# Two groups of four routed choices by 26 block products, in place of four pairs

## The chip, the cores and the metric

One core of a Trainium2 chip runs the kernel. Time is the device time of one execution in microseconds (us). The engines are named as in the profile: PE (TensorE, matmuls), PEld (its weight loads), DVE (VectorE), ACT (ScalarE), POOL (GpSimd) and SP (the queue that issues most DMAs). L738 means line 738 of the kernel before.

## The reference: what is computed

Sixteen batches of 256 rows and 256 columns pass two layers, each added to its input, all in float32.

- Layer 0: each batch takes the one expert of eight with the largest entry of `cond_8`: `silu(x Wu + bu) * (x Wg + bg)`, 512 wide, then back to 256 columns.
- Layer 1: each batch takes its two best experts of eight, weighted, and a shared one: `gelu(x Wg) * (x Wu)`, 1024 wide, then back to 256 columns.

```python
w, sel = jax.lax.top_k(softmax(router_logits), 2)
w = w / w.sum(axis=-1, keepdims=True)
...
out = sum over experts of we[:, None, None] * _gemma_mlp(x, g, u, d)
out = out + _gemma_mlp(x, shared_gate, shared_up, shared_down)
```

So layer 1 has 32 routed choices (16 batches, two each) and 16 batches for the shared expert.

## The kernel before

**Units.** The choices are sorted by expert on the chip, so that two neighbours of one expert form a *pair*. A `Pair` multiplies the expert's weights, cut in 2 x 2 blocks, with the two batches by seven block products in place of eight (`STEPS`, numbered 0 to 6). Its up part has four *quarters* (j = 0 to 3) in layer 1, each with seven products of two matmuls (gate and up, m = 0 and 1): 14 matmuls, at L753. Its down part has seven steps of four matmuls (L839), which are spread over the quarters of the next unit. A `Single` handles one choice without any scheme. A `Quad` handles four batches of one expert: its up part is two times 26 block products (`BLOCK`) of two matmuls, at L1126, and its down part is that of two pairs (its `halves`). Before the change only the shared expert's last twelve batches are done by quads, three of them; the other four shared batches are two pairs.

**Order in layer 1.** Two shared pairs, then the routed pairs (twelve that are always there, and up to four further ones, as many as the routing gives, chosen in a switch with one arm for each number), a single, the three quads, and the last single.

**A quarter of a pair.** Products 0, 2 and 4 sum in one PSUM bank, X. After each, ACT copies the bank to SBUF (u1, u2, u3; `copy`, L730), and PE may not add the next of them before the copy has read the bank. DVE combines such copies with the other banks into four blocks, C11 after product 1, C22 after 4, C21 after 5, and C12 after product 6, which is recorded in the next quarter (`combine`, L738). Then come GELU on ACT (L795), the product on DVE (L801), and three sums of the result on DVE (`sums_b`, L681 to L683). POOL makes four sums of each quarter's weights (`sums_a`, L688 to L691) three quarters ahead into `s` buffers, and once in a pair four sums of the down weights. POOL also issues the DMAs that add results to `out` (L650). SP loads weights (`q`) five quarters ahead.

**The written order.** All instructions are recorded in an order fixed by hand: a clock advances two units for each of the first six products of a quarter (`line.main`), so twelve units make a quarter, and `line.later(n, f)` records `f` when the clock has gone n units on. What falls due between two products is recorded between them, on whatever engines it uses. Each engine runs its own instructions in that order and waits by semaphores for others.

**Preparation.** A quad needs 26 factors for each half of the weights: P0 to P3 (blocks), Q0 to Q3 (blocks plus multiples of them, `RATIOS` = -1, 0, 1, 2), and for each two i < j a W (difference of two Q over the difference of their ratios) and two N (a block less W). `prepare()` makes them once, for the shared expert, among the routed pairs, and writes them to DRAM (`factors`), from where the quads load them. Its pieces are recorded 5 clock units into quarters j = 0 and 1 of the pairs after the first: `load` brings 1 MB of weights into the tile `spare` (L1326), `sums_w` makes Q (POOL, L1336), `pair` makes W and two N (POOL at L1346, L1350 and L1351, 256 elements wide; ACT scales W at L1349 where the ratios differ by more than one), `store` writes 128 KB at a time (L1321). The results pass through a ring of eight 256-wide pieces of the tiles `z`, `xs0` and `xs1`.

**Down weights of the quads.** All three quads use one expert's down weights `d` and their sums `ds` (L839 reads both), loaded once for the first of them.

**Sorting.** `order_by_expert` gives every choice a key, its expert times 32 plus its index; choices that are left over from pairs get 4096 more, and so come last.

Of the kernel before, what the change touches and what calls it, by code (L numbers as in the profile page):

```python
# [17 lines left out]
P = 128  # L18
# [6 lines left out]
NP2 = (NA - E) // 2  # L25
NS1, NS2 = B - 1 - 2 * NP1, NA - 2 * NP2
# [42 lines left out]
QUADS = (B - 2 * NF) // 4  # L69
# [5 lines left out]
def kernel(  # L75
# [22 lines left out]
    factors = [dram.tile([P, QW], F32, name=f"factors{j}") for j in range(CHUNKS)]  # L98

    qsums = [dram.tile([P, QW], F32, name=f"qsums{j}") for j in range(KPS[1])]  # L100
    dsums = dram.tile([P, 4 * KPS[1] * P], F32, name="dsums")
# [299 lines left out]
    def order_by_expert(v, g):  # L401
# [11 lines left out]
        odd, key, batch = map(small, ("odd", "key", "batch"))  # L413
        ri = small("ri", dt=I32)
# [31 lines left out]
        v.tensor_copy(ri, rank)  # L446
        v.tensor_single_scalar(ri, ri, 1, ALU.bitwise_and)
        v.tensor_copy(odd, ri)
        step(v)
        v.tensor_tensor(count, count, odd, ALU.add)  # L450
# [212 lines left out]
    class Pair(Unit):  # L663
# [41 lines left out]
        def sums_d(self):  # L705
            s = take("ds", 4, KPS[1], P, of=self)
            self.ds = s[:, :, : self.kp]
            flat = s.rearrange("p k j h -> p (k j h)")
            if self.at is None and self is not shared[0]:
                nc.sync.dma_start(flat, dsums)  # L710
                return
            d, s = self.d, self.ds
            self.sums_a(lambda n: d[:, A_AT[n]], lambda n: s[:, S_AT[n]])
            if self is shared[0]:
                nc.gpsimd.dma_start(dsums, flat)
# [236 lines left out]
    class Quad(Unit):  # L952
# [6 lines left out]
        def __init__(self, n, at, batches_at):  # L959
            super().__init__(n, 1, at, batches_at)  # L960
            self.kp = CHUNKS
            self.halves = [Pair(next(names), 1, at, batches_at[i : i + 2]) for i in (0, 2)]
# [3 lines left out]
        def load_q(self, j, behind=False):  # L966
            t = take("q", QB)[:, :QW]
            nc.sync.dma_start(t, factors[j])
# [58 lines left out]
        def load_d(self):  # L1027
            self.d = take("d", DW, of="quads")[:, : 4 * self.kd * P]
            src = wd1[bass.ds(self.expert(), 1)].rearrange("e p f -> (e p) f")
# [5 lines left out]
        def sums_d(self):  # L1035
            self.ds = take("ds", 4, self.kd, P, of="quads")
            nc.sync.dma_start(self.ds.rearrange("p k j h -> p (k j h)"), dsums)
# [55 lines left out]
        def down_over(self, h):  # L1093
# [3 lines left out]
            if h is self.halves[0]:  # L1097
                for sums in self.second:
                    sums()
            if not h.last:  # L1100
# [85 lines left out]
        def down(self, h, k):  # L1186
            h.d, h.ds = first_quad.d, first_quad.ds
            h.down(k)

    class Single(Unit):  # L1190
        width = 1

        def up(self, j):
# [31 lines left out]
            self.acts.append(act)  # L1225

        def down(self, j):
# [16 lines left out]
            if self.layer:  # L1244
# [7 lines left out]
                if self.x_from:  # L1252
# [13 lines left out]
        def piece(self, line, j, among=False):  # L1266
# [5 lines left out]
            if self.layer:  # L1272
                line.later(SINGLE_UP + 4 * bool(self.x_from), lambda: self.down(j))
# [34 lines left out]
    def prepare():  # L1308
# [3 lines left out]
        p = []  # L1312
        raw = {}
        ring = [areas["z"][:, i * S : (i + 1) * S] for i in range(4)]
        ring += [areas[f"xs{i}"][:, k * S : (k + 1) * S] for i in range(2) for k in range(2)]
        at = iter(range(1000))

        def store(g, name, src):
            n = g * len(BLOCK) + BLOCK.index(name)
            dst = factors[n // FACTORS][:, n % FACTORS * S : (n % FACTORS + 1) * S]  # L1320
            nc.sync.dma_start(dst.rearrange("p (m h) -> p m h", m=2), src)  # L1321

        def load(g):
            t = areas["spare"].rearrange("p (j m k h) -> p j m k h", j=2, m=2, k=4)
            for j in range(2):
                nc.sync.dma_start(areas["spare"][:, bass.ts(j, QW)], wq1[E, 2 * g + j])  # L1326
            for i in range(4):
                j, half = divmod(i, 2)
                raw["u", i], raw["w", i] = (t[:, j, :, 2 * half + c, :] for c in range(2))

        def sums_w(g):
            tt = nc.gpsimd.tensor_tensor
            for i, k in enumerate(RATIOS):
                w, u = raw["w", i], raw["u", i]
                for _ in range(abs(k)):
                    tt(w, w, u, ALU.add if k > 0 else ALU.subtract)  # L1336

        def store_w(g):
            for i in range(4):
                store(g, f"P{i}", raw["u", i])  # L1340
                store(g, f"Q{i}", raw["w", i])

        def pair(g, i, j):
            tt = nc.gpsimd.tensor_tensor
            t = [ring[next(at) % 8].rearrange("p (m h) -> p m h", m=2) for _ in range(3)]
            tt(t[0], raw["w", j], raw["w", i], ALU.subtract)  # L1346
            d = RATIOS[j] - RATIOS[i]
            if d != 1:
                nc.scalar.activation(t[0], t[0], AF.Copy, scale=1.0 / d)  # L1349
            tt(t[1], raw["u", i], t[0], ALU.subtract)  # L1350
            tt(t[2], raw["u", j], t[0], ALU.subtract)  # L1351
            raw[i, j] = t

        def store_pair(g, i, j):
            for name, t in zip((f"W{i}{j}", f"N{i}{j}", f"N{j}{i}"), raw[i, j]):
                store(g, name, t)

        for g in range(2):
            p += [[partial(load, g)], [partial(sums_w, g)]]
            ij = [(i, j) for i in range(4) for j in range(i + 1, 4)]  # L1360
            after = [partial(store_w, g)]
            for i, j in ij:
                p.append([*after, partial(pair, g, i, j)])
                after = [partial(store_pair, g, i, j)]
            p.append(after)
# [7 lines left out]
    quads = [Quad(next(names), None, range(i, i + 4)) for i in range(2 * NF, B, 4)]  # L1373
    first_quad = quads[0]
    first_quad.x_at = None
    pairs = [Pair(next(names), 1, 2 * i) for i in range(NP2)]
# [362 lines left out]
```

## Time and profile before

| | us |
|---|---|
| median of three runs | 1032.93 (1032.56 to 1033.51) |
| the profiled execution, whole | 1031.96 |
| its span in the trace | 1030.4 |
| PE busy in the span | 1022.7 (4714 matmul instructions) |
| DVE, POOL and ACT busy | 779.7, 499.3 and 384.5 |
| moved by DMA | 151.16 MB, 147 GB/s on average |

A row of a group reads: line, engine, operation, tile written <- tiles read, shapes (partitions x elements), count; then busy time, mean ns of one, and the engine's idle time just before with what ended it. A row of a timeline reads: start, length, engine, line, operation, tiles, count, and in brackets the idle time before it with what ended it. The granted clock of TensorE was full in every stage of this run.

### The profile page before, as it was taken

How to read it: one execution, taken by the hardware profiler on the slowest of the kernel's cores; microseconds unless marked ns; L12 is line 12 of the kernel's file. 1: busy time of each engine (PE TensorE's matmuls, PEld its weight loads, DVE VectorE, ACT ScalarE, POOL GpSimd, SP SyncE). 2: the span in 40 equal slices, each digit the busy share in tenths (PEclk: the TensorE clock that was granted, in tenths of full speed). 3: DMA queues.
4: the chain of work that ended last, by engine and by line, in shares of the span. 5: the costliest groups of instructions: out<-in, count | busy, mean ns of one | idle time of the engine just before them, and what ended most of it. 6: DMA issues, size and time to landing. Idle time of an engine off the chain costs nothing.

```text
span 1030.4 us, 14361 instructions
## 1 busy us (share of the span) xinstructions
PE 1022.7 (99%) x4714; PEld 894.1 (87%) x4714; DVE 779.7 (76%) x1265; ACT 384.5 (37%) x626; POOL 499.3 (48%) x558
## 2 busy tenths in 40 slices
PE   9999999999999999999999999999999999999998
PEld 7888888888888888888888888888888888888887
DVE  7888998777778778777887777777752897787661
ACT  2444443333333333333333333333331563543310
POOL 3929842455866977785887557647300000000001
PEclk9999999999999999999999999999999999999999
DMA  7635657552572464365346415423445653643324
GB/s 238 236 106 188 232 194 272 218 138 98 154 199 98 118 174 140 130 176 164 107 118 174 106 60 175 132 102 103 132 139 139 203 184 102 164 123 96 114 47 76
DMA packets 70027, 151.16 MB, mean 147 GB/s; under 512 B 8114, under 2 KB 39730, under 8 KB 66994
## 3 DMA queue, kind: packets, MB, share of 16 engines
q1 hardware_dynamic: 56674, 134.61, 38.6%
q0 software_dynamic: 12976, 15.21, 10.0%
q8 instruction: 42, 0.69, 0.3%
q14 instruction: 47, 0.39, 0.1%
q10 hardware_dynamic: 288, 0.26, 0.1%
HBM read 119.13 MB, written 30.93 MB: 146 GB/s over the span
## 4 chain that ended last, share of the span: by engine, by line
PE 96%; DVE 2%; DMA 1%; ACT 0%; issue 0%; SPq 0%; DVEq 0%
PE bank L753 46%; PE bank L839 31%; PE bank L1126 13%; PE bank L1199 4%; PE bank L1232 2%; DMA bt<-x_dram 1%; DVE c L738 1%; PE bank L231 1%; DVE bt L801 0%; DVE bt L681 0%; ACT c L789 0%; DVE bt L682 0%; PE bank L424 0%; ACT cp L730 0%; ACT c L795 0%
## 5 line engine op out<-in xcount | busy, mean ns | idle before, releaser
L730 ACT ACTIVATE cp<-bank 128x512 f32<-128x512 f32 x246 | 146.6, 596 | 382.7 <-PE bank L753 382.7
L753 PE MATMUL bank<-xt,s 128*128 128x256 f32 x1088 | 257.6, 380 | 0.4 <-DVE c L738 0.4
L738 DVE TENSOR_TENSOR c<-cp,bank 128x512 f32<-128x512 f32 x328 | 212.2, 679 | 26.2 <-ACT cp L730 16.2
L753 PEld LDWEIGHTS bank<-xt,s 128*128 128x128 f32 x1088 | 206.7, 190 | 29.2 <-DVE c L738 1.1
L753 PE MATMUL bank<-xt,q 128*128 128x256 f32 x816 | 195.8, 379 | 0.0
L650 POOL DMA_DIRECT2D out_dram<-ys x46 | 49.7, 1172 | 301.1 <-DVE ys L875 183.3
L839 PE MATMUL bank<-bt,ds 128*128 128x256 f32 x800 | 192.6, 380 | 0.0
L753 PEld LDWEIGHTS bank<-xt,q 128*128 128x128 f32 x816 | 155.3, 190 | 20.8
L801 DVE TENSOR_TENSOR bt<-c 128x1024 f32<-128x1024 f32 x82 | 115.4, 1407 | 76.5 <-ACT c L795 76.0
L839 PEld LDWEIGHTS bank<-bt,ds 128*128 128x128 f32 x800 | 152.0, 190 | 21.1 <-issue 0.7
L839 PE MATMUL bank<-bt,d 128*128 128x256 f32 x564 | 135.1, 379 | 0.0
L839 PEld LDWEIGHTS bank<-bt,d 128*128 128x128 f32 x564 | 107.3, 190 | 14.4
L688 POOL TENSOR_TENSOR s<-q 128x256 f32<-128x256 f32 x78 | 78.6, 1008 | 74.3 <-PE bank L753 45.2
L691 POOL TENSOR_TENSOR s<-s,q 128x256 f32<-128x256 f32 x78 | 66.8, 857 | 66.7 <-PE bank L753 64.0
L681 DVE TENSOR_TENSOR bt<-bt 128x512 f32<-128x512 f32 x101 | 81.3, 805 | 2.5 <-DMA bt<-x_dram 2.4
L689 POOL TENSOR_TENSOR s<-s,q 128x256 f32<-128x256 f32 x78 | 76.3, 978 | 6.1
L1126 PE MATMUL bank<-xt,q 128*128 128x256 f32 x336 | 77.0, 380 | 0.2 <-DVE ds L1151 0.2
L690 POOL TENSOR_TENSOR s<-q 128x256 f32<-128x256 f32 x78 | 74.0, 949 | 0.2 <-PE bank L753 0.2
L795 ACT ACTIVATE c<-c 128x1024 f32<-128x1024 f32 x68 | 71.5, 1051 | 6.8 <-DVE c L738 6.8
L1126 PEld LDWEIGHTS bank<-xt,q 128*128 128x128 f32 x336 | 63.8, 190 | 9.3 <-DVE ds L1151 0.6
L1126 PE MATMUL bank<-s,q 128*128 128x256 f32 x288 | 66.4, 379 | 0.0
L683 DVE TENSOR_TENSOR bt<-bt 128x256 f32<-128x256 f32 x94 | 61.4, 653 | 3.2
(225 smaller groups left out, 1121.2 us busy)
## 6 DMA issues: line engine op xcount, KB each, us to landing
q<-wq_dram SPq DMA_DIRECT2D x90, 512.0 KB, 3.7
q<-factors SPq DMA_DIRECT2D x39, 512.0 KB, 3.4
d<-wd_dram SPq DMA_DIRECT2D x17, 1024.0 KB, 5.8
xt<-x1d SPq DMA_DIRECT2D x46, 256.0 KB, 5.0
out_dram<-ys POOLq DMA_DIRECT2D x46, 256.0 KB, 5.8
d<-wd_dram SPq DMA_DIRECT2D x7, 513.0 KB, 3.8
bt<-x_dram SPq DMA_DIRECT2D x14, 256.0 KB, 5.1
x1d<-ys SPq DMA_DIRECT2D x14, 256.0 KB, 4.0
```

What stands on the lines that cost most here:

```text
L681: tt(more[:, 0:2, :], t[:, 0:3:2, :], t[:, 2:4, :], ALU.subtract)
L688: tt(s("S1"), a("A21"), a("A22"), ALU.add)
L689: tt(s("S2"), s("S1"), a("A11"), ALU.subtract)
L690: tt(s("nS3"), a("A21"), a("A11"), ALU.subtract)
L691: tt(s("nS4"), s("S2"), a("A12"), ALU.subtract)
L730: nc.scalar.activation(t, self.banks["X", j], AF.Copy)
L738: nc.vector.tensor_tensor(self.c[j][:, block].rearrange("p m s -> p (m s)"), self.copies[n, j], self.banks[tag, j], op,)
L753: nc.tensor.matmul(self.banks[tag, j][:, bass.ts(m, S)], lhsT=self.q[j][:, m, A_AT[a], :] if a in A_AT else self.s[j][:, m, S_AT[a], :], r ...
L795: nc.scalar.activation(u, u, AF.Gelu_apprx_tanh)
L801: nc.vector.tensor_tensor(t[:, 0:4, :], u, v, ALU.mult)
L839: nc.tensor.matmul(d, lhsT=src[:, j, :], rhs=self.act_block(j, b), start=OPENS[k] and j == 0, stop=j == self.kp - 1, skip_group_check=True,)
L1126: nc.tensor.matmul(dst[:, bass.ts(m, S)], lhsT=w[:, m, :], rhs=rhs, start=fresh and m == 0, stop=True, skip_group_check=True,)
```

## The change

Of the 32 routed choices, `NR` = ceil((32 - 3 x 8) / 4) = 2 groups of four of one expert become quads, in place of four of the twelve fixed pairs; eight fixed pairs stay. The sort puts choices that belong to a whole group of four first (their keys get 4096 less).

The factors of three experts are prepared now: those of the two routed quads and those of the shared quads. A preparation step does two index pairs at once, (01, 23), (02, 13), (03, 12), in operations on 512 elements where one cut serves both, and the difference that makes W moves from POOL to DVE; the scaling stays on ACT, the N on POOL. The ring has four pieces of 512. The pieces are recorded in five of every six quarters of all routed pairs, the step `two` 3 units into the quarter and stores 11 units in, and they run on into the further pairs of the switch. For the routed quads `prepare` also makes the sums of their down weights (`dsums`).

The routed quads come right before the shared ones. After the down steps of a routed quad, `d` and `ds` are given back and loaded for the next. The single before the quads takes its x into an `s` buffer, since `xs0` and `xs1` are the ring.

The diff, cut to its core:

```diff
-NP2 = (NA - E) // 2
+NR = -(-(NA - 3 * E) // 4)
+NP2 = (NA - E) // 2 - 2 * NR
+PAIRED = 4 * NR + 2 * NP2
...
# order_by_expert
-        v.tensor_copy(ri, rank)
-        v.tensor_single_scalar(ri, ri, 1, ALU.bitwise_and)
-        v.tensor_copy(odd, ri)
-        step(v)
+        v.tensor_copy(ri[:, 0:1], rank)
+        v.tensor_tensor(ri[:, 1:2], count, rank, ALU.add)
+        for i, ones in enumerate((1, 3)):
+            v.tensor_single_scalar(ri[:, i : i + 1], ri[:, i : i + 1], ones, ALU.bitwise_and)
+        v.tensor_copy(part, ri)
+        step(v)
+        v.tensor_tensor(full, count, full, ALU.subtract)
+        v.tensor_scalar(full, full, 0.0, -4096.0, ALU.is_gt, ALU.mult)
+        g.tensor_tensor(key, key, full, ALU.add)
...
# Quad
+            self.set = -1 if at is None else at // 4
+            self.factors = factors[self.set]
...
         def load_d(self):
+            turns["d"].sort()
             self.d = take("d", DW, of="quads")[:, : 4 * self.kd * P]
...
# Quad.down_over
+            if h is self.halves[1] and self in routed:
+                give("d", "quads")
+                give("ds", "quads")
+                after = quads[quads.index(self) + 1]
+                after.load_d()
+                after.sums_d()
...
# prepare
-        ring = [areas["z"][:, i * S : (i + 1) * S] for i in range(4)]
-        ring += [areas[f"xs{i}"][:, k * S : (k + 1) * S] for i in range(2) for k in range(2)]
+        ring = [areas["z"][:, : 2 * S], areas["z"][:, 2 * S :], areas["xs0"], areas["xs1"]]
+        twos = [t.rearrange("p (n m h) -> p n m h", n=2, m=2) for t in ring]
+        raw = areas["spare"].rearrange("p (j m a c h) -> p j a c m h", j=2, m=2, a=2, c=2)
+        gp, half = nc.gpsimd.tensor_tensor, ((0, 0), (0, 1), (1, 0), (1, 1))
...
-        def pair(g, i, j):
-            tt = nc.gpsimd.tensor_tensor
-            t = [ring[next(at) % 8].rearrange("p (m h) -> p m h", m=2) for _ in range(3)]
-            tt(t[0], raw["w", j], raw["w", i], ALU.subtract)
-            d = RATIOS[j] - RATIOS[i]
-            if d != 1:
-                nc.scalar.activation(t[0], t[0], AF.Copy, scale=1.0 / d)
-            tt(t[1], raw["u", i], t[0], ALU.subtract)
-            tt(t[2], raw["u", j], t[0], ALU.subtract)
-            raw[i, j] = t
+        def sums_w():
+            w, v = raw[:, 1, :, 1], raw[:, 1, :, 0]
+            gp(w, w, v, ALU.add)
+            gp(w[:, 1], w[:, 1], v[:, 1], ALU.add)
+            w, v = raw[:, 0, 0, 1], raw[:, 0, 0, 0]
+            gp(w, w, v, ALU.subtract)
+        def two(t, k):
+            sub = lambda engine, *aps: engine.tensor_tensor(*aps, ALU.subtract)
+            left, right = (raw[:, :, i] if k == 1 else raw[:, i] for i in range(2))
+            cuts = [(slice(None), slice(None))] if k < 3 else [(0, 1), (1, 0)]
+            for a, b in cuts:
+                sub(nc.vector, t[0][:, a], right[:, b, 1], left[:, a, 1])
+            if k > 1:
+                of = t[0] if k == 2 else t[0][:, 0]
+                nc.scalar.activation(of, of, AF.Copy, scale=1.0 / k)
+            sub(nc.gpsimd, t[1], left[:, :, 0], t[0])
+            for a, b in cuts:
+                sub(nc.gpsimd, t[2][:, a], right[:, b, 0], t[0][:, a])
...
+        for u in quads[: NR + 1]:
+            for g in range(2):
+                add(5, load, u, g)
+                p.append([])
+                add(5, sums_w)
+                add(11, store_w, u, g)
+                for k, ij in enumerate((((0, 1), (2, 3)), ((0, 2), (1, 3)), ((0, 3), (1, 2))), 1):
+                    t = [twos[(at + i) % 4] for i in range(3)]
+                    at += 3
+                    p.append([])
+                    add(3, two, t, k)
+                    add(11, store_two, u, g, t, ij)
+                p.append([])
+            if u in routed:
+                add(5, load_d, u)
+                p.append([])
+                add(5, sums_d)
+                add(11, store_d, u)
+                p.append([])
...
-    quads = [Quad(next(names), None, range(i, i + 4)) for i in range(2 * NF, B, 4)]
+    routed = [Quad(next(names), 4 * i) for i in range(NR)]
+    quads = [*routed, *(Quad(next(names), None, range(i, i + 4)) for i in range(2 * NF, B, 4))]
...
# Line.quarter
-            if unit in pairs[1:] and j < 2 and self.preparing:
-                for f in self.preparing.pop(0):
-                    self.later(5, f)
+            if self.preparing and (unit in pairs or unit in more_pairs or unit in ones):
+                self.skipped = (self.skipped + 1) % 6
+                for after, f in self.preparing.pop(0) if self.skipped else ():
+                    self.later(after if unit.width == 2 else after // 2, f)
+                if not self.preparing:
+                    self.later(12, lambda: turns["d"].append(2))
...
             for u in left[-1:]:
                 u.x_from = "at"
-            turns["xs"], turns["d"] = [0, 1], [*turns["d"], 2]
+            for u in left[:-1]:
+                u.x_from = "s"
```

## The prediction

> **What bounds the kernel now.** I read the page first: the busy line, then the chain of work that ended last, then the groups.
>
> ```profile
> span 1030.4 us, 14361 instructions
> ...
> PE 1022.7 (99%) x4714; PEld 894.1 (87%) x4714; DVE 779.7 (76%) x1265; ACT 384.5 (37%) x626; POOL 499.3 (48%) x558
> ...
> PE 96%; DVE 2%; DMA 1%; ACT 0%; issue 0%; SPq 0%; DVEq 0%
> ...
> L681 DVE TENSOR_TENSOR bt<-bt 128x512 f32<-128x512 f32 x101 | 81.3, 805 | 2.5 <-DMA bt<-x_dram 2.4
> L1126 PE MATMUL bank<-xt,q 128*128 128x256 f32 x336 | 77.0, 380 | 0.2 <-DVE ds L1151 0.2
> L795 ACT ACTIVATE c<-c 128x1024 f32<-128x1024 f32 x68 | 71.5, 1051 | 6.8 <-DVE c L738 6.8
> ```
>
> TensorE is the bound: 99% busy and 96% of the chain. So a matmul that goes is a gain in full, and every wait of TensorE is a loss in full; other engines count only through such waits. The 68 GELUs of L795 are four for each layer-1 pair: 17 pairs run (12 fixed, 3 of the counted further ones, 2 shared), then two singles and three groups of four.
>
> The mean of 380 ns holds the overlap of one matmul with the next. The pace is read from the timeline of PE, whose first two numbers are start and length, around the start of the third group of four:
>
> ```profile
> 911.08 3.62 PE L1126 MATMUL bank<-xt,q 128*128 128x256 f32 x16
> 914.87 3.80 PE L1126 MATMUL bank<-xt,q 128*128 128x256 f32 x16 [0.17 <-DVE ds L1151]
> 918.51 1.03 PE L1126 MATMUL bank<-s,q 128*128 128x256 f32 x4
> ```
>
> Where nothing waits, 8 instructions take 1.727 us from start to start (the next fence), 0.2159 each. Here 16 took 3.79 and then 3.64 instead of 3.454: the place cost 0.52 us, though the idle column says 0.17.
>
> Then the timelines of one quarter of a pair, PE, ACT and DVE. It is a third quarter (j = 2).
>
> ```profile
> 452.65 1.89 PE L753 MATMUL bank<-xt,q 128*128 128x256 f32 x8
> 454.38 1.89 PE L753 MATMUL bank<-xt,s 128*128 128x256 f32 x8
> 456.10 1.89 PE L839 MATMUL bank<-bt,ds 128*128 128x256 f32 x8
> 457.83 1.89 PE L753 MATMUL bank<-xt,s 128*128 128x256 f32 x8
> ```
>
> ```profile
> 453.71 0.60 ACT L730 ACTIVATE cp<-bank 128x512 f32<-128x512 f32 x1 [2.80 <-PE bank L753]
> 456.36 0.60 ACT L730 ACTIVATE cp<-bank 128x512 f32<-128x512 f32 x1 [2.05 <-PE bank L753]
> ```
>
> ```profile
> 453.39 1.40 DVE L681 TENSOR_TENSOR bt<-bt 128x512 f32<-128x512 f32 x1
> 454.83 1.37 DVE L682 TENSOR_TENSOR bt<-bt 128x256 f32<-128x256 f32 x1
> 456.24 0.84 DVE L683 TENSOR_TENSOR bt<-bt 128x256 f32<-128x256 f32 x1
> 456.99 1.27 DVE L738 TENSOR_TENSOR c<-cp,bank 128x512 f32<-128x512 f32 x2
> ```
>
> PE's rows are products 0 and 1; product 6 of the quarter before and product 2; a down step; products 3 and 4. Products 0, 2 and 4 sum in one bank, and ACT copies it after each: u1 at 453.71, u2 at 456.36 to 456.96. Product 4 may not start before u2 is out; it started at 457.83 + 0.86 = 458.69, so u2 has 1.73 us to spare. DVE's first combine (C11) needs product 1 (done by 453.71 + 0.86 = 454.57) but came at 456.99: DVE was 2.42 us late, held up by its own sums.
>
> Last, the windows, for POOL in pairs without preparation and for DMA at its fullest (columns: length, then PE, PEld, DVE, ACT and POOL busy, clock, DMA share, GB/s):
>
> ```profile
> 545.20:726.50 181.30, 181.30 (x841) 159.83 (x841) 136.60 (x197) 63.86 (x101) 110.27 (x108) 1.00 0.42 121
> ```
>
> ```profile
> 20.00:40.00 20.00, 20.00 (x93) 16.95 (x92) 15.98 (x31) 7.31 (x14) 18.92 (x26) 1.00 0.94 304
> ```
>
> **Matmuls removed.** Two pairs do 2 x 4 x 14 = 112 up matmuls, a group of four 52 x 2 = 104; the down steps are the same 56. Each matmul is two instructions in the profile (three groups: 3 x 104 x 2 = 624 = x336 + x288 of L1126). Two groups for four pairs save 2 x 8 x 2 = 32 instructions: 32 x 0.2159 = **-6.91 us**, all on the bounding engine. Two whole groups always exist: 32 choices over 8 experts leave at most 3 x 8 = 24 outside of groups.
>
> **More passages from group to group.** A group whose predecessor's down steps end in its face meets the 0.52 us shown above: at its start DVE still does the predecessor's late sums. Before, one passage was of that kind (the first group has no down steps beside it, so the second starts clean); after, five groups make three. Two more at 0.52: **+1.04**. From 0 (the other passage shows no idle) to twice that, since the weighted results of the new groups take 0.48 us each on DVE where the shared ones take 0.42.
>
> **The scaling on ACT moves in front of u2.** Preparation ran 5 clock units into a quarter, behind u2; the subtraction was POOL's, and POOL was ahead. Now `two` runs 3 units in. DVE's order becomes C11, subtraction, C12; ACT's u1, scaling, u2. For k = 2 and 3 the scaling waits for DVE, behind it on ACT stand u2 and the GELU, and TensorE's product 4 waits for u2. The new end of u2, from the start of u1: 0.86 + DVE's lateness + 0.68 (C11) + 0.82 (subtraction) + 0.60 (scaling; L730's row, same width) + 0.60 (u2) + 0.10 for hand-offs = lateness + 3.66; product 4 stands at 458.69 - 453.71 = 4.98. So TensorE loses lateness - 1.32. For k = 3 only the first 256 columns are scaled and one half-subtraction precedes: 0.70 and 0.41 in place of 0.82 and 0.60, lateness - 1.63.
>
> The 0.82 is the mean of L681 (512 wide, both inputs in SBUF) among the pairs, where it ran from 0.68 to 1.70; L738, with one input in a bank, never left 0.67 to 0.69. The Trainium skill ("GPSIMD Engine Reference", Specifications) states that GpSimd shares its SBUF interfaces with VectorE and that VectorE instructions with two SBUF inputs contend there, which the spread of L681 agrees with. It speaks against this change, which gives VectorE such an operation and GpSimd wider ones; it states no price, and by it the scaling would be late more often than I count.
>
> DVE's lateness at C11 in the eight pairs that carry preparation now, read off the timelines as above, is 0.47 us on average at j = 0, 1.51 at j = 1 (0.82 to 2.24), 2.24 at j = 2 (1.56 to 3.11), 0.45 at j = 3. Chunks run in five quarters of six, which puts the twelve scalings three to each j: at j = 1 one k = 2 and two k = 3, at j = 2 two k = 2 and one k = 3. Averaging lateness minus threshold over the eight values of each j (negative counted as none) gives 0.26 and 0.09 at j = 1, 0.92 and 0.63 at j = 2: 0.26 + 2 x 0.09 + 2 x 0.92 + 0.63 = 2.91, with the stray late j = 0 **+3.0 us**. Below, it is 0 if the lateness stays as at j = 3; above, 12 x 0.92 = 11.0 if it is everywhere as at j = 2. I take 3.0, as the phases of the quarter stay the same.
>
> **What I cost at nothing, and its cover.** POOL: 110.27 of 181.30 us without preparation, 61%. New, per set: twelve 512-wide and eight 256-wide operations, two sets also four 512-wide sums of the down weights; at 1.47 and 1.0 us (rows of L688 to L691) 3 x 25.6 + 2 x 5.9 = 89 us over 41 quarters of 9.07 us, 24%: 85% in all. POOL's sums run three quarters ahead, 27 us of cover. Its new waits (for DVE's subtraction, for stores of the ring) hold back those sums and the result DMAs, not TensorE. DVE's subtraction for k = 1 waits for `sums_w`, a quarter earlier; behind it stand the combines; if POOL were over 5 us late there, TensorE would follow. SP: some 130 more issues of 0.33 to 0.46 us, stores that wait for POOL and hold the weight loads behind them, which run five quarters (45 us) ahead. DMA: about 27 MB more than 151; at 304 GB/s in the first 40 us TensorE did not wait. The d and ds of a group are reloaded between groups: the last reader of d is followed by some 34 matmuls (14.7 us) before its next, ds by 30 (13 us); 1 MB lands in 5.8 us, two in a row in about 11. If that cover went, the worst landing on the page for half a megabyte (7.4 us) would put ds at 30 us, 17 late, twice. The added routing operations are six small ones in a stage with one wait of 0.43: 0 to 0.3.
>
> **Sum.** -6.91 + 1.04 + 3.0 = -2.87. The profiled execution took 1031.96 (span 1030.4 and 1.56 around it): 1029.09. The median of the three runs, 1032.93, stands 0.97 above it: **1030.1**.
>
> **Rivals.**
> - Nearly the whole gain: u2 never late, because the subtraction meets a POOL that stands waiting for it. For it: lateness of 0.45 at half of the places. -6.91 + 1.04: 1027.1. Chance 0.22.
> - Gain eaten: scalings cost 4 to 8 us in all, 0.33 to 0.67 each; for it, j = 2 shows 0.92. -1.9 to +2.1: around 1033. Chance 0.14.
> - Slower: the same wait everywhere. POOL at 85% contends with DVE's sums before every C11, and all twelve scalings lose 0.92: -6.91 + 1.04 + 11.0 = +5.1, 1038. It decides from 0.49 us each (5.87 / 12); slower by over 0.2% from 0.66. Against it: j = 0 and 3 recover fully today. Chance 0.15.
> - The reload of d and ds late, or DVE held by `sums_w`: two places at 5 us and more, 1036 to 1064. Chance 0.05, for the covers counted above.
>
> **Chances.** The forecast, scalings at 1 to 4 us, has 0.44 (1028.1 to 1031.1), of which 0.04 falls within 0.2% (2.07 us, about what a measurement of this kernel can tell from no change). Faster: 0.22 + 0.40 = 0.62; within: 0.04 + 0.14 = 0.18; slower: 0.15 + 0.05 = 0.20. The range goes from 1026.8, the full gain with a little less at the passages, to 1036.0, inside the slower case, so that about 0.15 is left out.
>
> **What would show it.** Right: PE x4682, L1126's line at 1040 instructions, up matmuls of pairs 448 fewer, down matmuls as many as before; idle time of the pairs' up matmuls put down to ACT's copy, in quarters j = 1 and 2 with a scaling, 2 to 4 us together; three passages with a wait for DVE. Wrong: no such idle time (the first rival), idle time at j = 0 and 3 too (the slower one), waits for d or ds at the down steps, or for POOL's s.

## The result, and the profile after

The changed kernel took 1035.06 us (median of 20 runs, 1033.61 to 1037.01) against 1032.57 (20 runs, 1031.45 to 1033.51): ratio 1.0023, 95% interval 1.0016 to 1.003. It is slower, by a little over the 0.2% that the prediction took for the least a measurement of this kernel can tell. The profiled execution took 1035.11 us. Its page:

```profile
span 1033.5 us, 14486 instructions
...
PE 1019.0 (99%) x4682; PEld 885.5 (86%) x4682; DVE 823.5 (80%) x1331; ACT 399.8 (39%) x656; POOL 468.0 (45%) x503
...
PE 80%; DVE 14%; issue 3%; ACT 2%; DMA 1%; SPq 0%; DVEq 0%; ACTq 0%
...
L764 PE MATMUL bank<-xt,s 128*128 128x256 f32 x832 | 198.9, 381 | 4.5 <-ACT cp L741 2.8
...
L1150 PE MATMUL bank<-xt,q 128*128 128x256 f32 x560 | 128.9, 380 | 0.6 <-DVE ds L1175 0.6
```

The 32 matmul instructions are gone (4714 to 4682), yet the span is 3.1 us longer, and the chain has 14% on DVE where it had 2%. Lines have moved: the copy L730 is L741, the combine L738 is L749, the up matmul L753 is L764, the product L801 is L812, the sums L681 to L683 are L692 to L694, POOL's L688 to L691 are L699 to L702. New are L1371 (the differences, DVE's and POOL's) and L1378 (the scaling). TensorE's waits:

```profile
PE bank L764 <- ACT cp L741: 2.8, 5, 0.9
...
PE bank L764 <- DVE c L749: 1.5, 2, 1.0
PE bank L1259 <- DMA spare<-wd_dram: 0.9, 1, 0.9
PE bank L1150 <- DVE ds L1175: 0.6, 3, 0.2
```

Waits understate what was lost, as the prediction showed at a passage. I therefore add up, over all successive matmuls, how far the distance from start to start exceeds 0.2158 us. By stage, in us ("start" is layer 0 and the two shared pairs, "pairs" the routed pairs, "end" from the last matmul's start to the end of the span; "lateness" is that of DVE at C11, averaged over the pairs from the second routed one on, eight of them in the kernel before and nine in the others):

| kernel | start | pairs | passages | last single's d | end | span | lateness |
|---|---|---|---|---|---|---|---|
| before | 8.21 | 0.00 | 0.52 | 0 | 5.02 | 1030.36 | 1.17 |
| before, again (c1) | 7.81 | 0.00 | 0.52 | 0 | 5.12 | 1030.06 | 1.19 |
| after | 7.96 | 6.39 | 1.68 | 1.17 | 6.61 | 1033.52 | 2.20 |
| after, again (c0) | 8.21 | 6.45 | 1.68 | 0 | 6.92 | 1032.99 | 2.20 |

After minus before: -6.91 (32 x 0.2158) + 6.39 + 1.16 + 1.17 - 0.25 + 1.59 = +3.15, and the spans differ by 3.16. So the loss sits in the routed pairs, where before there was none. Of the 6.39, 4.95 falls into seven of the twelve quarters with a scaling, 1.26 where the switch begins, with DVE 3.97 us late there, and 0.2 elsewhere. By what TensorE waits for, there are two kinds. 4.63 stands at product 4, in the seven quarters, which then starts 0.14 or 0.15 us after the copy u2 ends. The other 1.76 (0.32 of it in one of the seven quarters) stands at product 6, which adds to the bank that DVE reads for C22, and starts 0.15 us after C22 ends. One quarter (j = 2, k = 2), by the timelines of PE, ACT, DVE and POOL (excerpts):

```profile
382.77 1.89 PE L764 MATMUL bank<-xt,s 128*128 128x256 f32 x8
384.50 1.89 PE L850 MATMUL bank<-bt,ds 128*128 128x256 f32 x8
386.22 1.03 PE L764 MATMUL bank<-xt,s 128*128 128x256 f32 x4
388.17 1.10 PE L764 MATMUL bank<-xt,s 128*128 128x256 f32 x4 [0.92 <-ACT cp L741]
```

```profile
382.11 0.60 ACT L741 ACTIVATE cp<-bank 128x512 f32<-128x512 f32 x1 [2.80 <-PE bank L764]
386.90 0.63 ACT L1378 ACTIVATE z<-z 128x512 f32<-128x512 f32 x1 [4.20 <-DVE z L1371]
387.44 0.58 ACT L741 ACTIVATE cp<-bank 128x512 f32<-128x512 f32 x1
```

```profile
382.36 1.38 DVE L693 TENSOR_TENSOR bt<-bt 128x256 f32<-128x256 f32 x1
383.77 1.37 DVE L694 TENSOR_TENSOR bt<-bt 128x256 f32<-128x256 f32 x1
385.06 0.67 DVE L749 TENSOR_TENSOR c<-cp,bank 128x512 f32<-128x512 f32 x1
385.66 1.16 DVE L1371 TENSOR_TENSOR z<-spare 128x512 f32<-128x512 f32 x1
```

```profile
381.70 1.75 POOL L700 TENSOR_TENSOR ds<-ds,d 128x512 f32<-128x512 f32 x1
383.42 1.44 POOL L701 TENSOR_TENSOR ds<-d 128x512 f32<-128x512 f32 x1
384.82 1.45 POOL L702 TENSOR_TENSOR ds<-ds,d 128x512 f32<-128x512 f32 x1
```

ACT copied u1 at 382.11, then stood 4.20 us for the subtraction of L1371; only then came the scaling and behind it u2, at 387.44 instead of some 2.65 us after u1. Product 4 started at 388.17 where its turn was 386.22 + 0.86 = 387.08. DVE came to C11 at 385.06, 2.1 us late. Its sums, two of 1.4 us, are why: see POOL's rows beside them. The first (L693) ended at 383.74, 0.29 us after POOL's L700 (383.45); the second at 385.14, 0.28 after POOL's L701 (384.86).

That is a rule of the whole trace, not of this place. I took all 80 (before) and 78 (after) sums of the lines L682 and L683 (now L693 and L694) between 255.1 and 545.2 us. But for one, each takes one of three times: 0.42 us where no POOL operation overlaps it, about 0.83 behind one of 256 elements, 1.37 behind one of 512; and 116 of the 117 longer ones end 0.28 to 0.29 us after a POOL operation ends. Before had 28, 42 and 10 of the three kinds, after 13, 42 and 23. What stands in the way is mostly not the new work itself: of the 23, 15 wait behind POOL's sums of down weights for the pairs (L699 to L702 into ds), which the kernel before also makes (10 there), six behind the other 512-wide sums of the preparation, and two behind the differences of L1371. A fuller POOL pauses less, so its old operations meet DVE's: of the longer sums, 40 stand behind the old sums of weights before and 51 after, 12 and 13 behind the preparation. But the slowest kind grew by 13, and eight of these stand behind the preparation's own operations, which before, 256 wide, cost a sum 0.83 us at most; so the width adds to it.

The Trainium skill ("SBUF — State Buffer", SBUF: two separate sides) states that the port pair which VectorE and GpSimd share is locked: whichever starts first, a GpSimd operation or a VectorE operation with two SBUF inputs (this only against a GpSimd operation that reads SBUF), has it for the whole instruction, and the other is blocked until then. The rows agree for VectorE's side, by the 116 of 117 above; what POOL loses behind DVE I did not count.

The same stretch in the windows (columns as in the prediction), before and then after:

```profile
255.10:545.20 290.10, 290.10 (x1346) 255.75 (x1345) 227.93 (x313) 103.70 (x166) 220.58 (x220) 1.00 0.50 144
```

```profile
255.10:545.20 290.10, 286.54 (x1320) 249.97 (x1320) 255.91 (x326) 103.31 (x166) 248.76 (x230) 1.00 0.66 199
```

POOL went from 76% to 86% busy, DVE from 79% to 88%. DVE's groups there, before and after:

```profile
L738 DVE TENSOR_TENSOR c<-cp,bank 128x512 f32<-128x512 f32 x128 | 82.4, 679 | 7.8 <-ACT cp L730 5.4 <-PE bank L753 1.3 <-DVE bt L683 0.8
L801 DVE TENSOR_TENSOR bt<-c 128x1024 f32<-128x1024 f32 x32 | 44.6, 1394 | 35.5 <-ACT c L795 35.5
...
L682 DVE TENSOR_TENSOR bt<-bt 128x256 f32<-128x256 f32 x32 | 24.3, 761 | 1.1
```

```profile
L749 DVE TENSOR_TENSOR c<-cp,bank 128x512 f32<-128x512 f32 x128 | 82.5, 676 | 1.5 <-ACT cp L741 1.4
L812 DVE TENSOR_TENSOR bt<-c 128x1024 f32<-128x1024 f32 x31 | 51.8, 1671 | 25.3 <-ACT c L806 25.3
...
L693 DVE TENSOR_TENSOR bt<-bt 128x256 f32<-128x256 f32 x32 | 29.1, 909 | 1.1
```

The product, whose inputs are both in SBUF, went from 1394 to 1671 ns, the sum from 761 to 909; the combine, which reads a bank, stayed at 676 (before 679).

### The profile page after: what moved, and what is told of

It reads as the page before. It is cut to its first block, busy times and chain, and to the rows that moved or that the text cites. A ratio compares the mean times of both kernels' runs of the same rounds, so it can differ in the third digit from the quotient of the medians.

```text
span 1033.5 us, 14486 instructions
## 1 busy us (share of the span) xinstructions
PE 1019.0 (99%) x4682; PEld 885.5 (86%) x4682; DVE 823.5 (80%) x1331; ACT 399.8 (39%) x656; POOL 468.0 (45%) x503
## 4 chain that ended last, share of the span: by engine, by line
PE 80%; DVE 14%; issue 3%; ACT 2%; DMA 1%; SPq 0%; DVEq 0%; ACTq 0%
PE bank L764 28%; PE bank L850 26%; PE bank L1150 20%; DVE c L749 4%; DVE bt L812 2%; PE bank L1224 2%; PE bank L1259 2%; DVE bt L692 2%; DVE bt L693 2%; ACT c L806 1%; DMA spare<-wd_dram 1%; ACT cp L741 1%; DVE ys L882 1%; DVE xt L692 1%; DVE xt L693 0%
## 5 line engine op out<-in xcount | busy, mean ns | idle before, releaser
L741 ACT ACTIVATE cp<-bank 128x512 f32<-128x512 f32 x198 | 117.7, 594 | 262.4 <-PE bank L764 262.0
L764 PE MATMUL bank<-xt,s 128*128 128x256 f32 x832 | 198.9, 381 | 4.5 <-ACT cp L741 2.8
L764 PEld LDWEIGHTS bank<-xt,s 128*128 128x128 f32 x832 | 156.8, 190 | 30.2 <-issue 4.7
L749 DVE TENSOR_TENSOR c<-cp,bank 128x512 f32<-128x512 f32 x264 | 171.4, 677 | 12.7 <-ACT cp L741 8.9
L764 PE MATMUL bank<-xt,q 128*128 128x256 f32 x624 | 149.7, 379 | 0.0
L812 DVE TENSOR_TENSOR bt<-c 128x1024 f32<-128x1024 f32 x66 | 99.9, 1513 | 45.8 <-ACT c L806 45.3
L764 PEld LDWEIGHTS bank<-xt,q 128*128 128x128 f32 x624 | 118.6, 190 | 16.0
L1150 PE MATMUL bank<-xt,q 128*128 128x256 f32 x560 | 128.9, 380 | 0.6 <-DVE ds L1175 0.6
L1150 PEld LDWEIGHTS bank<-xt,q 128*128 128x128 f32 x560 | 105.9, 190 | 16.6 <-DVE ds L1175 1.8
L1150 PE MATMUL bank<-s,q 128*128 128x256 f32 x480 | 111.1, 379 | 0.0
L1150 PEld LDWEIGHTS bank<-s,q 128*128 128x128 f32 x480 | 91.3, 190 | 12.3
L699 POOL TENSOR_TENSOR s<-q 128x256 f32<-128x256 f32 x62 | 64.2, 1036 | 45.2 <-PE bank L764 23.4
L692 DVE TENSOR_TENSOR bt<-bt 128x512 f32<-128x512 f32 x95 | 77.7, 818 | 1.2 <-DMA bt<-x_dram 1.1
L702 POOL TENSOR_TENSOR s<-s,q 128x256 f32<-128x256 f32 x62 | 57.3, 924 | 21.7 <-PE bank L764 21.5
L694 DVE TENSOR_TENSOR bt<-bt 128x256 f32<-128x256 f32 x88 | 62.9, 714 | 3.0
L700 POOL TENSOR_TENSOR s<-s,q 128x256 f32<-128x256 f32 x62 | 60.5, 976 | 4.9
L693 DVE TENSOR_TENSOR bt<-bt 128x256 f32<-128x256 f32 x88 | 59.9, 681 | 3.0
```

Of the source, the lines that this page charges most:

```text
L692: tt(more[:, 0:2, :], t[:, 0:3:2, :], t[:, 2:4, :], ALU.subtract)
L693: tt(t2, t[:, C22, :], more[:, 0, :], ALU.add)
L694: tt(more[:, 2, :], t[:, C21, :], t2, ALU.subtract)
L699: tt(s("S1"), a("A21"), a("A22"), ALU.add)
L700: tt(s("S2"), s("S1"), a("A11"), ALU.subtract)
L702: tt(s("nS4"), s("S2"), a("A12"), ALU.subtract)
```

## The experiments

My theory W: the loss in the pairs is ACT's scaling, which waits for DVE with u2 behind it. Its second half, that DVE is late because POOL, with the wide differences in its queue, runs beside its sums, was at first rival C, and I took it over when the first runs had shown that the scaling is not all. The rivals: POOL alone, the amount of work, the groups themselves, and places outside the pairs. Each result gives the median in us of the run and of the kernel before, run beside it, then the ratio with its 95% interval; "pairs" and "lateness" are the columns of the table.

**The change once more.** No edit (c0).

> The changed kernel unaltered, as the yardstick of this call: about 1035.1 us against 1032.6 before (1.0023). Theory W (the scaling ahead of u2): the same three kinds of loss on TensorE as in the first profile, some 5 us before product 4 in quarters with a scaling, 1.7 us at three passages between groups, 1.2 us at the last single's first down step. Rival E (the end of the program): if the 1.6 us by which the span after the last matmul was longer belongs to the kernel, it is there again (6.6 us from the last matmul's start to the end of the span, against 5.0 before); if not, it varies from run to run.

1034.5 against 1032.29, ratio 1.0024 (1.0013 to 1.0036). The pairs lose 6.45 again, the passages 1.68; the last single's d lost nothing here. That term comes and goes: among the runs below it is 1.28 (e13), 1.07 (e12), 0.70 (e10), 0.43 (e11), 0.38 (e1), 0.13 (e9) and 0 in the others.

**The step later, behind u2.**

```diff
-                    add(3, two, t, k)
+                    add(5, two, t, k)
```

> The step two is recorded 5 units into the quarter instead of 3, so ACT's scaling stands behind the copy u2; the subtraction stays on DVE. Theory W: the 4.95 us lost before product 4 in the eight quarters that have a scaling go, about 1030.1 us (0.9976 of before). Rival C (DVE is late because it and POOL contend, and TensorE waits for DVE wherever the work stands): the time stays at 1034 to 1036, and the losses move to banks that DVE has not released.

1034.32 against 1032.29, 1.0019 (1.001 to 1.0028); pairs 6.44. The simple move cures nothing, as rival C had it: nothing is lost at product 4 any more (the expectation counted eight such quarters; they were seven), but the scaling now stands ahead of the GELU, and all nine losses stand at product 6. ACT's waits of L1378 among the pairs fell by a third only (they were 21.2 and 17.0 us), and TensorE now waits for DVE (4.5 us, nine times) where it had waited for ACT:

```profile
ACT xs L1378 <- DVE xs L1371: 13.9, 6, 3.6
...
ACT z L1378 <- DVE z L1371: 11.7, 5, 3.4
```

**No scaling.** The scaling of W for k = 2 and 3 is left out.

```diff
-            if k > 1:
-                of = t[0] if k == 2 else t[0][:, 0]
-                nc.scalar.activation(of, of, AF.Copy, scale=1.0 / k)
```

> The scaling of W on ACT is left out (the factors for k = 2 and 3 are not divided), everything else stays at 3 units. Theory W: as with the scaling moved, about 1030.1 us. Rival C: DVE's subtractions and POOL's work are still there, 1034 to 1036. Between: if only part of the 5 us goes, the rest is DVE's.

1030.85 against 1032.29, 0.9986 (0.9977 to 0.9995); pairs 3.00, lateness still 2.22, though POOL's differences wait for no scaling here. The 4.63 at product 4 is gone whole, but the loss at product 6 grew from 1.76 to 3.00. So half of the loss in the pairs goes, and what remains waits for DVE:

```profile
PE bank L764 <- DVE c L749: 2.1, 4, 0.8
```

**One set instead of three.** The preparation of the routed sets is left out; all groups read the shared factors.

```diff
-            self.factors = factors[self.set]
+            self.factors = factors[-1]
...
+        p += [[] for _ in range(12 * NR)]
-        for u in quads[: NR + 1]:
+        for u in quads[NR : NR + 1]:
```

> The preparation for the two routed experts is left out; their groups use the shared expert's factors and sums of down weights, and the shared set is prepared in the same quarters as in the changed kernel. Theory W: the losses of the shared set's scalings (0.60, 0.97 and 0.75 us in the profile) stay, those of the other two sets (2.6 us) and the 1.26 us at the switch go: about 1031.2 us. Rival G (the groups themselves lose what they save: passages, reload of d and ds, the last single): 1033 to 1035.

1030.43 against 1032.29, 0.9982 (0.9973 to 0.9991); pairs 2.12, lateness 1.35 (most of its quarters carry no preparation; in the four with a scaling it is 2.05). A third of the steps, a third of the loss: it comes by the step. These factors are not the right ones for the routed groups; the work on them is the same.

**The step in two.** The subtraction 5 units in, behind C12 on DVE; scaling and POOL's differences 9 units in, behind u3 on ACT.

```diff
+        def sub_two(t, k):
+            ...
-                    add(3, two, t, k)
+                    add(5, sub_two, t, k)
+                    add(9, two, t, k)
```

> DVE's subtraction at 5 units (just ahead of the product, where DVE waits for the GELU), ACT's scaling and POOL's two differences at 9 units (behind GELU and the copy u3). Theory A (the round trip DVE to ACT in the middle of a quarter costs, because ACT waits for the subtraction and either u2 or the GELU stands behind it): pair losses fall from 6.4 us to 1 to 2.5, the time to 1029.0 to 1030.5 (0.997 to 0.998 of before). Rival C (DVE's load and contention alone): pair losses of 3 us as without scaling, 1031, or more.

1028.08 against 1032.53, 0.996 (0.9947 to 0.9974): faster than both kernels. Its page:

```profile
span 1025.6 us, 14484 instructions
...
PE 92%; DVE 6%; ACT 1%; issue 1%; DMA 0%; SPq 0%; DVEq 0%; ACTq 0%
...
L764 PE MATMUL bank<-xt,s 128*128 128x256 f32 x832 | 197.1, 380 | 0.6 <-DVE c L749 0.6
```

The pairs lose 0.39, though DVE's lateness is 2.12, as in the changed kernel. Among ACT's longest waits in the pairs the scaling (here L1384) is no longer there:

```profile
ACT cp L741 <- PE bank L764: 176.0, 98, 2.8
ACT dz L875 <- PE bank L850: 29.7, 28, 1.1
ACT c L806 <- DVE c L749: 10.8, 12, 2.4
```

So a mean lateness of 2.1 us need not cost anything. It is not harmless everywhere: e2, with no scaling at all and the same lateness, lost 3.00 at product 6.

**No groups of routed choices** (`NR = 0`; the new form of preparation stays, for the shared set).

> NR = 0: no routed groups, twelve fixed pairs as before; the shared set is prepared with the wide operations, DVE's subtraction and the scaling at 3 units, and written in the first quarters of the routed pairs. 4714 matmul instructions. Theory A: the four scalings of one set cost 1 to 3 us of pair losses, so 1033.5 to 1035.5; the end is 5.0 us long if the groups' code makes it longer, else 6.6. Rival: the wide preparation costs nothing for one set, 1032.5.

1034.19 against 1032.53, 1.0017 (1.0008 to 1.0026); pairs 1.16, passages 0.52 as before, end 5.61. The preparation's new form costs something even for one set.

**The subtraction back on POOL**, the step 5 units in.

```diff
-                sub(nc.vector, t[0][:, a], right[:, b, 1], left[:, a, 1])
+                sub(nc.gpsimd, t[0][:, a], right[:, b, 1], left[:, a, 1])
...
-                    add(3, two, t, k)
+                    add(5, two, t, k)
```

> The subtraction goes back to POOL, all of two at 5 units, as the preparation before did, in the wide form. Theory A: ACT's scaling now waits for POOL, which was ahead before; with POOL some 6 per cent fuller it may be late at j = 2, behind the sums of the down weights: pair losses 1 to 5 us, 1029.5 to 1033. Rival C: DVE is rid of its twenty-four subtractions, so pair losses of less than 1.5 us, about 1029.5.

1032.72 against 1032.53, 1.0002 (0.9993 to 1.0012); pairs 4.15, lateness 2.51. Better than e1, where the pairs lost 6.44, and worse than e4: DVE is late without the subtraction too, when POOL has more.

**Subtraction at 3, the rest at 9** (as e4, with `add(3, sub_two, t, k)`).

> As the run with the subtraction at 5 and the scaling at 9 units, but with the subtraction at 3, ahead of C12. It tells the place of the subtraction from the place of the scaling. Theory A1 (the scaling's wait in ACT is the whole cost): as there, pair losses under 0.6 us, 1028.1. Theory A2 (the subtraction ahead of C12 costs too, since C12 feeds the GELU and the GELU the product): as in the run without scaling, pair losses of 2 to 3 us, about 1030.5.

1028.81 against 1032.49, 0.9973 (0.9962 to 0.9984); pairs 0.66. Nearly all comes from moving the scaling and POOL's differences away from the middle of the quarter, not the subtraction; e10 moves POOL's alone.

**Only POOL's differences at 9**, subtraction and scaling at 3.

> Subtraction on DVE and scaling on ACT at 3 units as in the changed kernel, only POOL's two differences moved to 9 units. With the changed kernel (all at 3: pair losses of 6.5 us), the run without scaling (3.0) and the run with the scaling and POOL at 9 (0.66), it separates the scaling's place from POOL's. If the scaling ahead of u2 is the cause, the losses before product 4 stay at 3 to 5 us: 1031.5 to 1033.5. If POOL's contention with DVE at 3 units is, they fall under 1.5 us: about 1029.5.

1035.32 against 1032.33, 1.0026 (1.0015 to 1.0038); pairs 6.53, of it 5.52 at product 4; the time lies above both forecasts. While the scaling stands ahead of u2, POOL's place changes nothing. Once it is out of the way, POOL's place counts: e2 (no scaling, POOL at 3) lost 3.00 and e7 (scaling and POOL at 9) 0.66, at nearly the same lateness (2.22 and 2.11).

**No differences.** POOL's two N differences of each step are left out; W is stored in their places.

```diff
-            sub(nc.gpsimd, t[1], left[:, :, 0], t[0])
-            for a, b in cuts:
-                sub(nc.gpsimd, t[2][:, a], right[:, b, 0], t[0][:, a])
```

> POOL's two differences (the N factors) are left out; W is stored in their places. Subtraction and scaling stay at 3 units. It tests what made DVE late at C11, 2.2 us on average in the changed kernel against 1.17 before: if POOL's work beside DVE's sums, the lateness falls to 1.2 to 1.5 us and the pair losses to the 3 us that the prediction worked out from 1.17, about 1030.8; if DVE's own subtraction and its waits, it stays near 2 us and the time at 1033 to 1034.5.

1027.9 against 1032.33, 0.9958 (0.9944 to 0.9971); pairs 0.67, lateness 1.37, with the scaling where the change put it. The lateness fell as the first theory had it (in the twelve quarters with a scaling from 1.85 to 1.07), the loss to far less than its 3 us; the prediction's formula, worked out quarter by quarter below, accounts for it. The windows and DVE's sum:

```profile
255.10:545.20 290.10, 290.04 (x1343) 254.59 (x1343) 241.43 (x330) 105.78 (x170) 210.97 (x199) 1.00 0.67 199
```

```profile
L693 DVE TENSOR_TENSOR bt<-bt 128x256 f32<-128x256 f32 x32 | 25.8, 807 | 1.1
```

Of DVE's 80 sums, counted as above, 31 now take 0.42 us and 11 take 1.37. Both halves of W stand: with scaling and differences moved behind u3 the lateness does hardly any harm (e4), and without POOL's differences the scaling does little (e11).

**Narrow differences.** The same work of POOL in operations on 256 elements.

```diff
-            sub(nc.gpsimd, t[1], left[:, :, 0], t[0])
-            for a, b in cuts:
+            for n in range(2):
+                sub(nc.gpsimd, t[1][:, n], left[:, n, 0], t[0][:, n])
+            for a, b in ((0, 0), (1, 1)) if k < 3 else cuts:
```

> The changed kernel with POOL's two N differences of each step cut into operations on 256 elements instead of 512 (the same work in twice as many instructions); subtraction and scaling stay where the change put them. In the profiles so far, every 256-wide sum of VectorE among the pairs takes one of three times: 0.42 us where no POOL operation overlaps it, 0.83 where one of 256 elements does, 1.37 where one of 512 does, and the two slower ones end 0.28 us after the POOL operation ends. The changed kernel has 23 of the 1.37 kind, the kernel before 10, the kernel without the differences 11. If the length of the POOL operation is what makes VectorE late (theory: width): the 1.37 kind falls to about 11, mean lateness at C11 from 2.2 to 1.5 to 1.9, loss in the pairs from 6.4 to 2 to 4.5 us, time 1031 to 1033.5. If it is the amount of POOL's work (rival: volume): POOL is no less busy, sums of 0.83 take the place of those of 1.37 in larger number, lateness stays 2.1 to 2.3, loss 5.5 to 7, time 1034 to 1036.

1032.51 against 1032.52, 1.0004 (0.9995 to 1.0013); pairs 3.70, lateness 2.00. In the windows POOL is busier than in the changed kernel (248.76):

```profile
255.10:545.20 290.10, 288.12 (x1330) 251.37 (x1329) 253.26 (x326) 104.71 (x169) 255.49 (x251) 1.00 0.67 199
```

Time and loss are as the theory of width has them, the counts are not: 8, 52 and 19 sums of the three kinds, where some 11 of the slowest were expected, and only 8 of 79 take 0.42 us; the lateness lies between the two theories. In the twelve quarters with a scaling, lateness fell from 1.85 to 1.46 and the loss from 4.95 to 2.6. So the fullness of POOL keeps DVE late, and the width has a part in what that costs; how large a part one run does not settle.

**What is left outside the pairs.** Two versions of e4 tried to shorten the passages: the last down steps of a group earlier (`DOWNS_AT` ending in 46, 47, 48, 49), and the sums on ACT's place later (`ACT_SUMS_AT = 9`).

> Subtraction at 5, scaling at 9, and the last four down steps of a group two to four units earlier (46, 47, 48, 49 in place of 48, 48, 49, 50 in DOWNS_AT), so that DVE's sums for the next down part come before the next group starts. If the loss at a passage is DVE's lateness after those steps, the three passages fall from 0.58, 0.58 and 0.51 us to under 0.2 each: 1027.0. If DVE is late for another reason, they stay.

> Subtraction at 5, scaling at 9, and ACT_SUMS_AT 9 in place of 5: the sums of a finished block come four units later. If the sums that come due at the passage are what holds DVE there, the losses of 0.58, 0.58 and 0.51 us change place or shrink; if they wait for something else (a free buffer), nothing moves: 1028.1.

1028.5 and 1027.96 against 1032.49, both 0.996 (0.9946 to 0.9973). The first made the passages longer (1.89 in all), the second left them at 1.68. Neither shortened them.

For the end, one arm fewer in the switch, so that the arm taken is the last in the code:

```diff
-    MOST = ((NS1 - 1) // 2, NS2 // 2)
+    MOST = ((NS1 - 1) // 2, NS2 // 2 - 1)
```

> The changed kernel with one arm of the switch fewer (MOST[1] = 3 in place of 4; these inputs need 3), so that the arm that runs is the last one and its end branches over no other arm. It tests why ACT's first instruction after the switch comes 5.7 to 6.0 us after the last matmul where before it came at 4.1. Theory D (the code that the branch skips): 4.1 to 4.4 us, the span 1.3 to 1.9 us shorter, about 1033. Theory D2 (where ACT's code happens to lie): no change in that direction, 1034.5.

1033.06 against 1032.33, 1.0007 (0.9998 to 1.0017): end 5.16 instead of 6.61 and 6.92. That is as theory D has it, so the code that the last branch skips is the likely cause, but one profile does not show it: of the thirteen profiles whose end skips this arm the ends run from 5.58 (e11) to 6.97 (e6). That the longer end is the kernel's and not a run's, the kernel before bears out once more (c1, the row in the table, 1031.66 us):

> The kernel before, for a second profile of its end. Theory E1 (the longer end belongs to the changed program): again about 5.0 us from the last matmul's start to the end of the span, where the five profiles of the changed program and its variants show 6.5 to 6.9. Theory E2 (chance): anywhere from 5 to 7.

## Why the prediction was wrong, point by point

Against the sum for a profiled execution (1029.09) the measured 1035.11 is 6.02 too long: passages +0.12, pairs +3.39, last single's d +1.17, end +1.59, start -0.25. (The step from there to a median, +0.97 by three runs, was too large as well: by twenty runs it is +0.61 for the kernel before and -0.05 for the changed one.)

- **Matmuls removed: right.** PE x4682, and L1150 has 560 + 480 = 1040 instructions.
- **Passages: right.** +1.16 for +1.04, three of them, at 776.0, 845.7 and 915.3, each waiting for DVE.
- **The scaling ahead of u2: the right mechanism, the wrong size.** This is the step that failed: the term of +3.0 was 6.39 in the pairs, 4.63 of it at product 4. The wait is there, put down to ACT's copy, as the prediction asked; that its idle time of 2.8 us lies in the 2 to 4 that it named proves little, since that column understates the loss. Feed each quarter's lateness, measured in the changed kernel, into its own formula (lateness less 1.32 or 1.63) and it gives 5.5 for the 4.63. Put in each subtraction's own time too, and take off what one quarter had lost just before (0.32): now it gives 4.69, and none of the twelve quarters is off by more than 0.05. It fits the other profiles with the scaling at 3 units as well: 5.58 for 5.52 in e10, 0.71 for 0.67 in e11, 2.53 for 2.57 in e13. So the formula held. What was wrong was the input: the lateness of before, 0.48, 1.51, 2.24 and 0.45 for j = 0 to 3, became 1.91, 2.25, 2.84 and 1.79. "I take 3.0, as the phases of the quarter stay the same": they don't, because the change itself gives POOL work that holds DVE's sums up; without POOL's differences (e11) the mean was 1.37 in place of 2.20. The loss spread to j = 0 (0.34 and 0.60), which the prediction had named as the sign of its slower rival. The durations were right on average (the subtraction 0.84 for 0.82, the scaling 0.63 for 0.60), but the single whole subtractions ahead of a scaling took 0.68 us (four) or 1.16 (two), and the first halves 0.41 to 0.42 (five) or 0.89 (one).
- **The contention was named and not priced.** The prediction cited the shared interfaces as speaking against the change, said that the page gave no price, and left the term out of the sum; it stands only in the rival "slower", at a chance of 0.15. The price stood in the trace of before: 0.42, 0.83 and 1.37 us for one and the same sum, by the POOL operation beside it.
- **At nothing: POOL's load was right** (85% foretold, 86% measured), and the groups' d and ds and POOL's s were not late (no wait of a matmul is put down to them). **DVE was not free:** the waits at product 6, which the sum had at nothing, cost 1.76, most of it (1.26) where the switch begins.
- **SP was not free.** The last single's d is loaded into `spare`. SP waited 19.5 us instead of 10.7 for DVE (L1175, before L1151) to read what was there, issued the load at 985.72 instead of 976.58, and the first matmul that needs it waited. It cost 1.17 in one profile of the changed kernel and 0 in the other, where SP waited as long. PE's timeline, then SP's wait before and after:

```profile
992.51 1.97 PE L1259 MATMUL bank<-cp,spare 128*128 128x256 f32 x8 [0.93 <-DMA spare<-wd_dram]
```

```profile
SPq L613 <- DVE d L1151: 10.7, 1, 10.7
```

```profile
SPq L624 <- DVE ds L1175: 19.5, 1, 19.5
```

- **The end was not in the sum.** After the last matmul's start ACT branched out of the switch at 1.65 or 1.66 us in every profile; its next instruction came at 4.08 and 4.11 us in two profiles of before, at 5.72 and 6.03 in two of the changed kernel, at 4.26 with the arm taken as the last (e12), and between 4.66 and 6.07 in the other runs with groups.
- **The rivals.** The nearest was "gain eaten" (4 to 8 us in all, 0.33 to 0.67 each): 4.95 over twelve scalings is 0.41, and -6.91 + 1.16 + 6.39 = +0.64 would have been no change. The d and the end, neither of which I had priced, made it slower. Of these the end alone was there in both profiles. The time lies inside the range, on the other side of no change.

Open are: what makes the passages 0.55 each (two attempts missed), how DVE's lateness divides between the width and the amount of POOL's work, and why the changed kernel ends later than the one before, which also skips an arm; e12 only points to the skipped code.

## What to carry to other kernels

That GpSimd has time left does not make work added to it free: here it took away the pauses in which VectorE's operations with both inputs in SBUF ran undisturbed, so VectorE's lateness in the changed kernel has to be worked out anew and not read from the trace of before. Where a small step on a third engine waits for VectorE, ask what stands behind it in that engine's queue, and put it behind the last thing that TensorE needs: the same operations in another place turned 1.0023 into 0.996. And with TensorE 99% busy, price the end and the queue of loads too; they made 2.8 us of the profiled execution.

## What the runs showed of the hardware

The three durations of one 256-wide sum on DVE (0.42, 0.83 and 1.37 us), set by the POOL operation beside it and ending 0.28 us after that one, were sharper than I had thought contention to be. And from ACT's last branch to its next instruction 2.4 to 2.5 us passed in two profiles of before, 4.1 and 4.4 in two of the changed kernel, and 2.6 with no arm left to skip (e12), but 3.0 to 4.4 among the variants that skip the same arm as the changed kernel.
